# Folds on VectorE, four transposes a tile, smaller code and pair steps, and another passage between two passes

## The chip, the cores and the metric

The kernel runs on one core of one Trainium2 chip. The metric is the device time of one execution in microseconds (us); the time of a kernel is the median of its runs.

## What is computed

The input x holds 16 x 1024 = 16384 tokens of E = 512 numbers (f32). Cut to what matters:

```python
xn = layernorm(x)                                   # over the 512 numbers
# attention part: a circular filter, a 24-bit code, its correction
D    = fractal_dimension(xn)                        # from the first 1024 numbers
x1   = ifft(fft(xn) * wave_filter(D, E)).real
bits = sigmoid(x1 @ W_el + b_el) > 0.5              # 24 bits a token
syn  = (bits @ H.T > 0.5); w = syn.sum(-1)          # 12 checks
corrected = bits with the pattern of syn flipped if 0 < w <= 3
s    = x1 + corrected @ W_le + b_le
# expert part: top 2 of 8 experts
probs   = softmax(xn @ router_w.T)
v, idx  = top_k(probs, 2)
weights = v / (v.sum() + 1e-6)
f    = sum over the two of (xn @ expert_w[idx] + v) * weights
out  = x + s * silu(f)
```

## The kernel before, in words

Tokens are cut into NT = 128 tiles of 128 tokens. The kernel passes over them twice.

**First pass** (`pass_1`, a loop over tiles g). Blocks of TPT = 4 tiles (1 MB) are loaded by SP (`load_block`, L157) into a pool `xin` of 5 buffers, AHEAD_L = 16 tiles ahead. The circular filter has mirror symmetry, so a row is first folded: `fold` (L442 to L450) adds and subtracts the halves of a row (L445, into `halved`, with the second quarter written mirrored) and then subtracts two quarters (L448, into `folded`). The list `folds` says in which tile each of a block's three fold steps is issued, on VectorE (DVE). `transpose` (L528, L532) turns the folded rows on TensorE (PE): two pairs of transposes at L528 add up in PSUM, which does one more sum of quarters, and two at L532 turn `folded`; ScalarE (ACT) copies the result to `pmt` (L534). `filt` multiplies `pmt` with the filter `fw` (L542, four f32 matmuls of 128x162), ACT copies the filtered tile to `yb` (L548), and SP stores a block of them to `yd` (L556). `take` reduces the 34 small columns (24 latents, 8 logits, two sums) to `raw` (L472, DVE, one a tile). `spread` squares the row with a sum on ACT (L459). PE turns tile g+1 ahead of the filter of tile g.

Small operations follow the tiles. For each group of GT = 8 tiles `scale` (L488 to L510) works out mean and scale of the layernorm on DVE, ACT and one POOL copy; `code` (L567 to L622) forms the bits, turns them on PE (L576), gets the checks by a matmul (L585), corrects the first 12 bits and packs them into one integer. For each round of RT = 16 tiles `route` (L654 to L825) finds the two experts, their weights and bias, marks the pair among 28 (`pair`, L729, four products), counts tokens of each pair before this one by matmuls, and so the place of each token in its pair's list (L782, L787); then POOL (GpSimd) scatters one record a token to `lists` in DRAM (L791). These operations wait in Python lists (`scales`, `now`, `routes`, `rest`, `aside`); `pass_1` issues about one from each at fixed places in a tile, between the folds. `None` in a list skips a turn. After SOON = 80 tiles `whole_ops(0)` (L873 to L944) reads the lists of the first 30 whole tiles back.

**The passage.** `lead_x` (g = 118), `lead_normal` (g = 124) and `lead_turn` (g = 127) prepare the second pass's first tile inside the first pass. After the last tile come the last `take` and the last `scale`. Then the pools of the first pass close, and those of the second take their memory.

**Second pass** (a loop over n from -11). Tokens are now sorted by pairs of experts: 101 "whole" tiles of one pair each, 61 "item" tiles of one expert each for what is left over, 27 "rest" tiles that put these together. POOL gathers x and the filtered rows (`fetch_x`, `fetch_y`, L1082); `normalize` (L1267, DVE); then the tile is turned, the first six on PE (`turn`, L1276, copy L1278), the others by ACT copies and a DMA (L1283 to L1292). `product` (L1324) is four f32 matmuls of 128x512; a whole tile has two, one an expert, joined by `scaled` (L1381, ACT) and `added` (L1384 DVE, L1387 ACT). The corrected code goes through `triple` (L1339, L1340, DVE: a bit mask to 3 x 32 numbers), `turn_code` (L1354 PE, L1358 ACT) and `mend` (L1366 PE); `spread_out` (L1371 to L1378) unfolds the filtered row; `combine` (L1423, L1424) makes the output, which POOL scatters (`put`, L1433). The order is written out by hand: a table `due` says in which turn n of the loop each step of tile k is issued, all but the products in `beside`, which runs between the two products of a tile.

## Time and profile before

| what | us |
|---|---|
| median of 5 runs | 1384.13 |
| lowest and highest | 1370.68, 1396.9 |
| the profiled execution | 1377.58 |
| its span on the core | 1375.7 |
| PE busy | 1246.8 (91%) |
| DVE busy | 998.5 (73%) |
| ACT busy | 787.9 (57%) |
| POOL busy | 796.0 (58%) |
| last `raw` (L472) of the first pass starts | 302.70 |
| first product (L1324) starts | 312.79 |
| third product starts | 322.4 |

A group in the profile is written: line, engine, operation, output <- input by the program's names, partitions x elements, how often; then its busy time and the mean ns of one; then the idle time of its engine just before it and who ended that. PEld is the loading of PE's weights, which overlaps PE. "issue" is time in which an engine waited for nothing that the profile shows. The granted clock is the share of full speed that TensorE's throttle allowed. A chain of waits follows the end back through what released each step.

### The profile page before, as it was taken

To read this page: it belongs to the slowest core of one execution; us is meant where nothing else is said; L and a number is where in the kernel's file an instruction comes from. 1 tells how busy PE (TensorE), PEld (TensorE's weight loads), DVE (VectorE), ACT (ScalarE), POOL (GpSimd) and SP (SyncE) were. 2 spreads that over 40 slices of the span, in tenths; PEclk is the share of its full clock that TensorE was granted. 3 is DMA by queue.
4 is the path that set the end of the run, shared out by engine and by line. 5 is a ranking of instruction groups with operands and counts; after the bars stand their busy time and mean duration, and the time that the engine had idled before them with its cause. 6 is when DMAs were issued, how large, how long until landed. Compare 5 with 4: busy or idle time off the path is not lost.

```text
span 1375.7 us, 17149 instructions
## 1 busy us (share of the span) xinstructions
PE 1246.8 (91%) x4417; PEld 685.6 (50%) x4417; DVE 998.5 (73%) x2538; ACT 787.9 (57%) x1326; POOL 796.0 (58%) x764
## 2 busy tenths in 40 slices
PE   9999886967897999988989998999899999996997
PEld 8988886853342444433434433444344444442444
DVE  8899886763865799633323444699798999995996
ACT  7988886763433454554545555456465555553553
POOL 0065555346475375654566543577767777776761
PEclk9999999998898999998999999999999999997998
DMA  8888786544345465775788889779877798886871
GB/s 304 296 288 281 271 277 220 181 165 124 77 124 131 102 167 131 185 189 141 179 200 208 198 194 188 194 186 220 220 193 218 195 214 212 212 211 181 211 195 62
DMA packets 235640, 266.42 MB, mean 194 GB/s; under 512 B 182558, under 2 KB 183070, under 8 KB 227482
## 3 DMA queue, kind: packets, MB, share of 16 engines
q1 hardware_dynamic: 188330, 133.16, 37.9%
q0 software_dynamic: 46928, 132.03, 33.2%
q8 instruction: 40, 0.66, 0.2%
q14 instruction: 54, 0.44, 0.1%
q10 hardware_dynamic: 288, 0.13, 0.0%
HBM read 140.79 MB, written 83.56 MB: 163 GB/s over the span
## 4 chain that ended last, share of the span: by engine, by line
PE 37%; DVE 21%; issue 18%; POOL 7%; another core or an unknown queue 6%; DMA 5%; ACT 4%; SPq 0%; POOLq 0%; DVEq 0%; ACTq 0%
PE pe L1324 26%; PE py L542 6%; DMA plt<-pl 3%; DVE acc L1384 3%; DVE halved L445 2%; DVE yg L1371 2%; POOL xg L1082 2%; PE pt L528 2%; POOL entry L1082 2%; POOL out L1433 2%; DVE yg L1423 2%; DVE xn L1267 1%; DVE mix L1374 1%; PE pt L532 1%
## 5 line engine op out<-in xcount | busy, mean ns | idle before, releaser
L1324 PE MATMUL pe<-w_sb,xt 128*128 x2136 | 953.1, 599 | 28.8 <-ACT xt L1292 8.0
L1324 PEld LDWEIGHTS pe<-w_sb,xt 128*128 128x128 f32 x2136 | 408.1, 194 | 505.4 <-issue 455.8
L1292 ACT COPY xt<-plt 128x1024 uint16<-128x1024 uint16 x156 | 209.3, 1342 | 87.0 <-DMA plt<-pl 58.2
L791 POOL DMA_INDIRECT lists<-rec,dst x128 | 143.5, 1121 | 99.3 <-issue 67.9
L1387 ACT ACTIVATE acc<-acc,stats 128x512 f32<-128x512 f32 (+2 forms) x103 | 73.5, 714 | 217.6 <-DVE acc L1384 174.3
L542 PE MATMUL py<-fw,pmt 128*128 128x162 f32 x1024 | 169.5, 308 | 29.3 <-ACT pmt L534 16.7
L1433 POOL DMA_INDIRECT out<-xg,toks x100 | 112.1, 1121 | 131.1 <-DVE xg L1424 102.8
L542 PEld LDWEIGHTS py<-fw,pmt 128*128 128x128 f32 x1024 | 146.8, 192 | 39.7 <-ACT pmt L534 21.3
L1283 ACT COPY pl<-xn 128x1024 uint16<-128x1024 uint16 x156 | 162.0, 1038 | 0.0
L1384 DVE SCALAR_TENSOR_TENSOR acc<-pe,stats,acc 128x512 f32<-128x512 f32 (+2 forms) x103 | 75.9, 737 | 117.9 <-remote 52.7
L1395 DVE COPY part<-pe 128x512 f32<-128x512 f32 x61 | 42.0, 689 | 152.6 <-remote 82.1
L1082 POOL DMA_INDIRECT yg<-yd,toks x101 | 112.4, 1113 | 69.7 <-DVE xg L1424 26.6
L1381 ACT ACTIVATE acc<-pe,stats 128x512 f32<-128x512 f32 (+2 forms) x103 | 68.9, 669 | 119.5 <-remote 49.2
L1082 POOL DMA_INDIRECT xg<-in_x,toks x100 | 109.6, 1096 | 45.6 <-issue 31.1
L548 ACT COPY yb<-py 128x512 f32<-128x512 f32 x128 | 75.5, 590 | 35.0 <-PE py L542 14.2
L459 ACT ACTIVATE no<-xt 128x512 bf16<-128x512 f32 x128 | 92.5, 723 | 0.0
L1423 DVE TENSOR_TENSOR yg<-yg,acc 128x512 f32<-128x512 f32 (+1 forms) x130 | 87.9, 676 | 5.2 <-ACT acc L1387 5.2
L1424 DVE TENSOR_TENSOR xg<-yg,xg 128x512 f32<-128x512 f32 (+1 forms) x129 | 88.2, 684 | 4.5
L1082 POOL DMA_INDIRECT part<-ed,adr_r x54 | 61.0, 1130 | 40.8 <-DVE mix L1375 20.6
L445 DVE TENSOR_TENSOR halved<-xt 128x512 f32<-128x512 f32 (+1 forms) x136 | 82.7, 649 | 0.1
L534 ACT COPY pmt<-pt 128x512 f32<-128x512 f32 x128 | 73.9, 577 | 12.0 <-remote 5.9
L1082 POOL DMA_INDIRECT entry<-lists,adr_i x61 | 63.2, 1036 | 28.4 <-issue 18.3
(279 smaller groups left out, 1483.2 us busy)
## 6 DMA issues: line engine op xcount, KB each, us to landing
yd<-yb SPq DMA_DIRECT2D x32, 1024.0 KB
xt<-in_x SPq DMA_DIRECT2D x31, 1024.0 KB
ed<-part SPq DMA_DIRECT2D x61, 256.0 KB
w_sb<-in_expert_w SPq DMA_DIRECT2D x32, 256.0 KB
plt<-pl SPq DMA_TRANSPOSE x156
lists<-rec,dst POOLq DMA_INDIRECT x128
yg<-yd,toks POOLq DMA_INDIRECT x101
xg<-in_x,toks POOLq DMA_INDIRECT x100
```

What stands on the lines that cost most here:

```text
L445: op(to[:, :, ::-1] if q else to, x[:, :, a:z], x[:, :, H + a : H + z])
L459: nc.scalar.activation(no, x, AF.Square, bias=x[:, 0:1], scale=-1.0, accum_out=k.sq2[:, j : j + 1],)
L542: nc.tensor.matmul(blocks(py)[:, i // 2, i % 2, :], pmt[:, i, :], fw[:, i, :], start=True, stop=True,)
L791: dma = nc.gpsimd.indirect_dma_start(out=lists, out_offset=bass.IndirectOffsetOnAxis(ap=st.dst[:, j : j + 1], axis=0), in_=st.rec.bitcast( ...
L1082: nc.gpsimd.indirect_dma_start(out=dst, out_offset=None, in_=src, in_offset=bass.IndirectOffsetOnAxis(ap=idx, axis=0), bounds_check=limit - 1,
L1283: nc.scalar.copy(k.pl.rearrange("p (h e) -> p h e", h=2), k.xn.bitcast(U16).rearrange("p (e h) -> p h e", h=2),)
L1292: nc.scalar.copy(k.xt.bitcast(U16).rearrange("p c (t h) -> p h c t", h=2), k.plt.rearrange("p (h c) t -> p h c t", h=2),)
L1324: nc.tensor.matmul(pe[:, o].unsqueeze(1), k.xt[:, c, :], w_sb[:, bass.ds(e, 1), c, o], start=(c == 0), stop=(c == KC - 1),)
L1384: nc.vector.scalar_tensor_tensor(k.acc[:, c], src[:, c], k.w1, k.acc[:, c], ALU.mult, ALU.add)
L1423: nc.vector.tensor_mul(k.mix[:, c], k.mix[:, c], k.acc[:, c])
L1424: nc.vector.tensor_add(k.x[:, c], k.mix[:, c], k.x[:, c])
L1433: dma = nc.gpsimd.indirect_dma_start(out=of, out_offset=bass.IndirectOffsetOnAxis(ap=k.tok, axis=0), in_=k.x, in_offset=None, bounds_check ...
```

## The change

- **Folds.** Sum and difference of the halves are one operation each for a block (128x1024 instead of two of 128x512), not mirrored any more; the difference of quarters reads its second input mirrored; a fourth operation adds the quarters in place, which the two pairs of transposes did before. `transpose` is four plain ones. A block's folds are issued in four tiles.
- **Groups.** GT is 16, so scale, code and route all work on 16 tiles. `xin` has 4 buffers and loads are issued 12 tiles ahead. SOON is 64. Constants made on the chip (`iota_e`, `rev`) come as rows.
- **Code.** The matmul of the checks has a 13th column that gives the code word as a number; the checks are weighted so that their sum holds count and pattern; the correction is an exclusive or of two integers a token.
- **Route.** Equality with the largest and the rank are one operation; the pair comes from a sum of two marks compared with 28 keys (one `is_equal` of 128x448) instead of four products; the matrix of the rank has 2^22 on its diagonal, so that the place is a maximum instead of a product and a sum; the weights take fewer operations.
- **Budget.** A tile gets a credit of 2.1 (us) less 0.21; folds and small operations take from it, and small operations are issued while some is left.
- **Passage.** The triples of the first four tiles are formed in the first pass's last four tiles. The last group's scale moves from the end of the first pass to turn n = -5, behind `normalize` of the second tile, with its MEAN copy on ACT. `turn` of tile k is due at k - 1 (before: max(k - 3, min(k - 2, 3))), `turn_code` at max(k / 2, k - 3), with half turns placed between the second product and `added`. Every 15th gathered x uses the first tile's buffer.

```diff
-    SOON = 80
+    SOON = 64
-    xin = p1.enter_context(tc.tile_pool(name="xin", bufs=5))
+    xin = p1.enter_context(tc.tile_pool(name="xin", bufs=4))
...
-    GT = 2 * TPT
+    GT = 4 * TPT
-    AHEAD_L = 16
-    RT = 2 * GT
+    AHEAD_L = 12
+    STEP, LATE = 2.1, 2.1
+    RT = GT
...
         if i < 2:
             op = nc.vector.tensor_sub if i else nc.vector.tensor_add
-            for q in range(2):
-                a, z = q * Q, (1 + q) * Q
-                to = t[:, :, i * H + a : i * H + z]
-                op(to[:, :, ::-1] if q else to, x[:, :, a:z], x[:, :, H + a : H + z])
+            op(t[:, :, i * H : (i + 1) * H], x[:, :, 0:H], x[:, :, H:E])
         else:
             v = t.rearrange("p j (a h n) -> p j a h n", a=2, h=2)
-            nc.vector.tensor_sub(
-                h.rearrange("p j (a n) -> p j a n", a=2), v[:, :, :, 0, :], v[:, :, :, 1, :]
-            )
+            if i == 2:
+                nc.vector.tensor_sub(
+                    h.rearrange("p j (a n) -> p j a n", a=2), v[:, :, :, 0, :], v[:, :, :, 1, ::-1]
+                )
+            else:
+                nc.vector.tensor_add(v[:, :, :, 0, :], v[:, :, :, 0, :], v[:, :, :, 1, ::-1])
...
         for c in range(2):
-            for i, half in enumerate((t[:, c, 0, :], t[:, c, 1, :])):
-                nc.tensor.matmul(
-                    pt[:, c, :], half, ident, start=(i == 0), stop=(i == 1), is_transpose=True
-                )
+            nc.tensor.transpose(pt[:, c, :], t[:, c, 0, :], ident)
...
         def c0():
             o.syn = made("syn", 12)
-            nc.vector.tensor_scalar(o.syn, k.pg, 0.5, None, ALU.is_gt)
+            nc.vector.scalar_tensor_tensor(
+                o.syn, k.pg[:, :, 0:12], 0.5, worth_r.unsqueeze(1).to_broadcast([P, GT, 12]),
+                ALU.is_gt, ALU.mult,
+            )
...
         def c2():
+            o.word = made("word", 0, I32)
+            nc.vector.tensor_copy(o.word, k.pg[:, :, 12])
         def c3():
+            o.fix = made("fix", 0, I32)
+            nc.vector.scalar_tensor_tensor(o.fix, o.w, 4.0 * COUNT, o.w, ALU.is_lt, ALU.mult)
+        def c4():
+            nc.vector.tensor_scalar(o.fix, o.fix, COUNT - 1, None, ALU.bitwise_and)
+        def c5():
+            nc.vector.tensor_tensor(
+                k.rec.bitcast(I32)[:, :, BITS], o.fix, o.word, ALU.bitwise_xor
+            )
...
+        def pairs_():
+            st.oh = new("oh", [P, S, NPAIR], BF16)
+            v.tensor_tensor(
+                st.oh,
+                st.key.unsqueeze(2).to_broadcast([P, S, NPAIR]),
+                key_r.unsqueeze(1).to_broadcast([P, S, NPAIR]),
+                ALU.is_equal,
+            )
...
+        def where():
+            st.far = new("far", [P, S])
+            v.tensor_reduce(st.far, st.pk, AX.X, ALU.max)
         def place():
-            st.pl = new("pl", [P, S, NPAIR])
-            v.tensor_mul(st.pl, st.pk, st.oh)
...
+        def small_ops(n):
+            nonlocal credit
+            for _ in range(n):
+                going = False
+                for ops in (scales, routes, now):
+                    if credit <= 0 or not ops or ops[0] is None or id(ops) in waiting:
+                        continue
+                    if ops[0]() is False:
+                        waiting.add(id(ops))
+                        continue
+                    credit -= getattr(ops.pop(0), "us", 0.17)
+                    going = True
+                if not going:
+                    break
...
+            credit = min(credit, 0.4) + (STEP if g < NT - 16 else LATE) - 0.21
+            waiting.clear()
+            small_ops(1)
             while folds and folds[0][0] <= g:
-                fold(*folds.pop(0)[1:])
+                b, i, js = folds.pop(0)[1:]
+                fold(b, i, js)
+                credit -= 1.2 * (js.stop - js.start) / TPT
                 steps(rest, 1)
...
+            small_ops(99)
...
+            if g >= NT - 4:
+                n = len(lead.b3)
+                lead.b3.append(triple_of(masks[0][:, n : n + 1]))
...
-        for op in scales + scale(NG - 1):
+        for op in scales:
             op()
...
+        pool, name = (xgp, "xg") if (k.at - 1) % (XG + 1) else (own, "x0")
...
         "turn": [
-            None if crossed[k] else max(k - AHEAD_T, min(k - 2, 3)) for k in range(NTILE)
+            None if crossed[k] else k - 1 for k in range(NTILE)
         ],
-        "turn_code": [k - 3 for k in range(NTILE)],
+        "turn_code": [max(k / 2, k - 3) for k in range(NTILE)],
...
             each(n + AHEAD_N, normalize)
+            if n + AHEAD_N == 1:
+                for op in scale(NG - 1):
+                    if op:
+                        op()
```

## The prediction

> **What bounds the kernel now.** I read the page's forty slices first, then tables of busy time by stretch, then the groups of instructions by form inside a steady stretch, then the waits and the chain around the passage. The change touches the first pass and the few tiles after it, so the first question is who sets the pace there. Columns of the table: stretch and its length, then busy us (and instructions) of PE, PEld, DVE, ACT, POOL, then PE's granted clock, DMA share, GB/s.
>
> ```profile
> 16.00:45.00 29.00, 28.38 (x222) 27.29 (x221) 26.24 (x70) 27.71 (x67) 0.42 (x2) 1.00 0.85 318
> 45.00:145.00 100.00, 92.32 (x712) 86.99 (x711) 91.18 (x319) 89.27 (x228) 42.87 (x40) 1.00 0.85 289
> 145.00:217.00 72.00, 64.08 (x487) 59.59 (x486) 62.15 (x214) 60.14 (x154) 40.08 (x37) 1.00 0.80 272
> 217.00:265.00 48.00, 37.48 (x257) 33.93 (x256) 35.22 (x126) 31.08 (x78) 18.75 (x19) 0.89 0.59 205
> 265.00:303.00 38.00, 28.93 (x213) 25.99 (x211) 25.52 (x96) 28.15 (x72) 18.02 (x18) 1.00 0.34 119
> ```
>
> The same table of L472 alone (one instruction a tile) counts tiles: 16, 48, 32, 17, 16. So a tile takes 1.81, 2.08, 2.25, 2.82 and 2.38 us in the five stretches. In the second, PE, DVE and ACT are each busy 89 to 92 of 100: no engine alone is the bound, three that hand work to each other are. DMA moves 289 GB/s there and 318 in the stretch before, so it is not at its end. In the last two everything is slack: 33 tiles take 86 us where 2.08 each would be 69. The steady stretch by form:
>
> ```profile
> L542 PE MATMUL py<-fw,pmt 128*128 128x162 f32 x384 | 62.5, 305 | 5.3 <-ACT pmt L534 1.8 <-DVE dev L515 1.2 <-DVE athot L679 1.0
> ...
> L445 DVE TENSOR_TENSOR halved<-xt 128x512 f32<-128x512 f32 x49 | 31.4, 680 | 0.0
> L528 PE MATMUL pt<-ident,halved 128*128 128x128 f32 x190 | 29.0, 274 | 0.0
> ...
> L532 PE MATMUL pt<-ident,folded 128*128 128x128 f32 x96 | 18.3, 273 | 0.0
> ...
> L448 DVE TENSOR_TENSOR folded<-halved 128x1024 f32<-128x1024 f32 x12 | 14.6, 1216 | 0.0
> L472 DVE TENSOR_REDUCE raw<-py 128x34 f32<-128x136 f32 x48 | 14.1, 294 | 3.4 <-ACT yb L548 2.3 <-issue 1.1
> ```
>
> PE's idle time falls before the filter (L542), behind ACT and behind DVE's small operations; DVE has next to no idle time ahead of its folds. The passage, in the chain of waits:
>
> ```profile
> 301.98 6.26 DMA xg<-in_x,toks
> ...
> 311.56 0.85 PE pt L1276 x4
> 312.42 0.11 PE pc L1354
> 312.52 0.27 issue
> 312.79 5.79 PE pe L1324 x8
> ```
>
> and in the list of waits from 300 to 320:
>
> ```profile
> POOL xg L1082 <- ACT no L459: 14.1, 1, 14.1
> ...
> PE pc L1354 <- DVE b L1340: 8.7, 1, 8.7
> ```
>
> The last filter ends near 302, then PE stands 8.7 us, although its first product needs only tile 0, turned already: in PE's order tile 1's transposes and code words stand ahead of it. The rest, 312.8 to 1365, is products (L1324, 953 of the 1052 us), which the diff leaves alone past the first tiles.
>
> **The change part by part.** Profiled execution: 1377.6 us (span 1375.7 and 1.9 around it); the median of five is 1384.1, 0.5% above. I take gains against the former and set them off from the latter.
>
> *Folds on DVE.* A block of four tiles had four of 128x512 (680 ns) and one of 128x1024 (1216). It gets four of 128x1024. Neighbours on DVE overlap by about 0.08 us in the timeline (two L445 take 1.22, not 1.36). Before: 4 x 0.680 + 1.216 - 5 x 0.08 = 3.54; after: 4 x 1.216 - 4 x 0.08 = 4.54. So +1.00 a block, +4.0 us for 16 tiles. The mirrored read now sits on an input; the mirrored write of L445 shares a 1.22 us pair with a plain one, so I cost mirroring at nothing (bounds 0 to +0.2 us an operation).
>
> *Small operations on DVE, for 16 tiles, by rows.* Scale: two rounds of seven (0.170 + 0.174 + 0.162 + 0.159 + 0.136 + 0.166 + 0.419 = 1.39) become one with six of 0.17 and a 128x512 of 0.68: 2.77 to 1.70. Code: two of 2.01 (L567 to L622) become one of 0.55 (384 elements, from 351 ns at 192 and the folds' slope of 1.05 ns an element), 0.35, 0.35 and four of 0.17: 4.02 to 1.93. Route: 10.2 to 7.85; gone are the four pair products (0.88) for one is_equal of 128x448 (0.61), three operations of 0.28, one 0.61 product, seven of 0.17. Sum 17.0 to 11.5, and some 30 instructions fewer. Start to start (less 0.08 where they overlap) that is 13.0 to 8.6: -4.3 us, against +4.0 of the folds. DVE per tile stays where it was, 1.90 us, and -0.02 (bounds -0.06 to +0.06).
>
> *Transposes.* Six a tile become four. A steady tile's four L528 take 0.60 us and two L532 0.38 in the timeline, so one costs 0.11; PE falls by 0.22 us a tile, 1.94 to 1.72. ACT: half the scale and spread steps, -0.03 of 1.86.
>
> *What that makes of the pace.* 2.08 us is 0.14 above the busiest engine, because three are level. Now PE is 0.2 below, with DVE 1.89 and ACT 1.83 left. Lower bound 1.89 (DVE never waits); upper bound 2.08 (the waits for L548 and for dependent pairs stay). I take 2.00, since PE's own waits for DVE and ACT no longer pass on: -0.08 on 112 tiles = -9. The first sixteen, with no small operations, are DVE's loss: 26.24/16 = 1.64 + 0.25 = 1.89 against 1.81, with waits +2, and +0.5 in the setup's extra fold. In the slow stretches (23 us over 2.08 a tile) PE's lighter tile saves a sixth, -4. First pass: -11 (bounds -25, the slow stretches gone; +5, below).
>
> *Group of 16, credit.* One scale for 16 tiles comes at most 8 tiles later, records and scatters with it. POOL is busy 43 of 100 in the steady stretch, so its queue of scatters, the same 128, absorbs that; each is one L791 of 1.1 us. In code and scale the empty steps give PE and ACT a tile each, so waits like DVE's 3.7 us for L502 (six of 0.6) should go: inside the 2.00. The last group has no successor in the first pass; its scale now runs on DVE behind the second normalise, 1.2 us where DVE waits for gathers anyway (3.65 us at 308), and its MEAN copy moves from POOL's queue (0.22 between gathers) to ACT. POOL's order is else the same: 8 xg gathers, 6 yg, then the scatters.
>
> *Loads.* Blocks are issued 12 tiles ahead, not 16, with four buffers, so the slack before the first fold falls from 11 to 7 tiles: 14 us against a landing of some 7. Cover: that slack. If a landing takes over 14 us, DVE waits.
>
> *SOON 64.* The read-back of the lists comes 16 tiles earlier; 30 whole tiles are full there either way. Same operations: nothing.
>
> *Passage.* Tile 1's turn moves behind the first product; tile 0 to 3's masks (0.44 us each) go to the last four tiles, where DVE is busy 25.5 of 38. The first product then starts at the end of pass 1 (302.7) + 0.3, not +10.1; the second waits for turn(1): gather landed +6.3, normalise 0.65, transposes and copy 1.2, about +8; the third at +11.6, where it was at 322.4, +19.7. So -8. Later forward waits change place: normalise(6) now stands behind turn(2), a product later, and the third product's psum behind the first addition; -1 to +2. The stall from 326.5 (9.2 and 4.7 us on the chain, PE's completions late with no named cause) may go or stay: 0, bounds -14 and 0. I take -9 with the first product at full clock (3.6, not 5.79, while the second may pay that).
>
> The granted clock was 0.70 from 302.7 to 312.8, behind PE's 8.7 us stand, and the four matmuls of the first product took 3.78 us of 5.79 in their first half. [...]
>
> Sum: -11 - 9 = -20: 1357.6 by the profiled execution, 1364 by the median.
>
> **The rivals.**
> *DVE sets the pace, so fewer transposes buy nothing.* For: DVE is 91 of 100 busy already and gains nothing net. Against: its waits are on L548, behind PE. The pace stays 2.08, and only the passage (-9) and -1 remain: 1374.
>
> *The passage gives nothing.* Second and third product wait for something else (a psum buffer, the 326.5 stall grown by what was saved). For: 18% of the chain is issue time and 6% unnamed. Pass 1's -11 stays: 1373.
>
> *Slower: DVE's whole-block folds hold up the reduce.* Each fold is one 1.22 us instruction in three of four tiles before and in all four now; behind it stand L472 and the small operations, and PE's next filter waits for L472 to free py, of which there are two. If each fold makes the filter wait, a tile costs DVE's 1.89 plus the reduce's own chain, filter 1.27 to L548 0.59 (1.86 in series, half of it beside DVE at best): up to 2.3 us. It decides from where the pace passes 2.08 + 9/112 = 2.16; at 2.30 pass 1 costs +25, with the passage +16: 1400. For: L472's 3.4 us of waits are on that chain now. Against: in the second stretch, three of four tiles already hold 1.2 us of folds with PE 92% busy.
>
> *The slow stretches go.* 23 us in pass 1 and 14 in the passage stand over the pace; if they hang on PE being full, half more leaves: 1342.
>
> **How the numbers follow.** Chances: forecast 0.45 (1354 to 1373), DVE bound 0.18, no passage 0.11, slower 0.15, slow stretches gone 0.11. About 1% (14 us) is what the runs, 1371 to 1397, can tell from none: faster is below 1370, slower above 1398. Forecast's part under 1370 is 0.36 of 0.45, the last case 0.11, and 0.06 of the two middle ones: 0.53. Slower: 0.6 of its rival 0.15 and 0.04 of mishaps in the long second pass: 0.13. Same: 0.34. The range, 1343 to 1396, leaves out half of the last case and half of the slower one with a little. The forecast's own range is 1354 to 1373.
>
> **What would show it.** Steps of L472: 2.00 us a tile from 45 to 217, and about 1.9 in 16 to 45. Folds x128 at 1.22. Of the small operations some 30 fewer for 16 tiles. Four transposes taking 0.60, PE busy near 82 of 100, DVE over 92. DVE's waits for xt: none. First L1324 within 1 us of the last filter, third 12 us behind it, and pass 1's last L472 near 292. Wrong if L472's pace is 2.08 or more, if DVE waits for loads, if the third product still comes 19 us after the pass, or if the second pass (1053 us from first product to end) has changed length by more than the passage's share.

## The result: 0.8% slower, and the profile after

The changed kernel takes 1384.8 us (median of 52 runs, 1367 to 1403); the kernel before took 1378.0 beside it (94 runs, 1355 to 1403). The ratio is 1.0079, interval 1.0058 to 1.0099: about 11 us slower (6.8 by the medians), where 20 faster were forecast. Here and below a ratio and its interval go by the runs within about 1.5% of the kernel's fastest alone, a median by all runs, so that the two can differ (most for the old passage with early folds, where three of twelve runs count). The profiled execution has a span of 1383.6 us, 7.9 above the one of before.

By stage the profiles differ thus: the first pass ends (last `raw`) at 317.6 instead of 302.7, +15, and from there to the end it is 1066 us instead of 1073, -7. So the passage paid about as forecast, and the first pass, which was to end at 292, lost 15 where it should have gained 11. Busy time by stretch, of the kernel after (columns as before; the stretches hold 16, 32, 32, 16 and 24 tiles, and the last 8 tiles follow them):

```profile
18.30:52.50 34.20, 28.61 (x197) 26.68 (x197) 29.84 (x60) 26.91 (x65) 0.24 (x1) 0.95 0.61 225
52.50:123.00 70.50, 56.46 (x414) 51.08 (x414) 61.43 (x156) 58.73 (x146) 23.62 (x21) 1.00 0.77 273
123.00:197.00 74.00, 60.21 (x414) 55.18 (x413) 61.74 (x157) 59.21 (x146) 39.97 (x34) 0.93 0.74 262
197.00:248.50 51.50, 37.45 (x225) 33.66 (x225) 33.46 (x88) 29.94 (x74) 20.94 (x17) 0.80 0.54 186
248.50:297.00 48.50, 41.10 (x305) 37.78 (x304) 45.31 (x116) 43.58 (x111) 29.47 (x24) 1.00 0.82 272
```

The loads came out as worked out: in the second row DVE is busy 61.43/32 = 1.92 us a tile, PE 56.46/32 = 1.76. But a tile takes 2.20 us there and 2.31 in the next row, where the same 32 tiles took 2.08 and 2.23 before. DVE is 87% busy, not over 92: no engine is full, so the loss is waiting. Whose? Take the first pass as a whole, from the first `raw` to its end. Before, the kernel's row was

```profile
15.90:302.70 286.80, 251.29 (x1882) 233.90 (x1879) 240.12 (x822) 236.35 (x594) 119.84 (x114) 0.98 0.73 251
```

and after

```profile
18.30:318.00 299.70, 237.86 (x1636) 216.72 (x1635) 244.37 (x623) 231.40 (x571) 124.57 (x104) 0.94 0.68 238
```

PE works 13.4 us less and stands 61.8 us instead of 35.5: 26 us more of waiting swallow the lighter work and add 13; the other 2.4 of the 15 lie ahead of the first `raw`. The groups of the first pass, by form, say where PE stands; of the kernel after:

```profile
L532 PE MATMUL pt<-ident,halved 128*128 128x128 f32 x256 | 54.0, 295 | 37.7 <-DVE halved L455 24.8 <-DVE dst L801 4.8 <-DVE lohi L719 3.5
...
L477 DVE TENSOR_REDUCE raw<-py 128x34 f32<-128x136 f32 x128 | 37.6, 294 | 39.0 <-ACT yb L550 29.9 <-issue 8.6
```

and the same two operations before:

```profile
L528 PE MATMUL pt<-ident,halved 128*128 128x128 f32 x512 | 78.8, 277 | 0.0
...
L472 DVE TENSOR_REDUCE raw<-py 128x34 f32<-128x136 f32 x128 | 37.6, 294 | 32.6 <-ACT yb L548 21.3 <-issue 10.9
```

The first transposes of a tile never waited before; now PE stands 37.7 us in front of them, two thirds of it for L455, the new fourth fold (the quarters added in place). One such wait, in the timeline:

```profile
90.53 1.21 DVE L455 TENSOR_TENSOR halved<-halved 128x1024 f32<-128x1024 f32 x1
...
91.89 0.41 PE L532 MATMUL pt<-ident,halved 128*128 128x128 f32 x2 [1.85 <-DVE halved L455]
...
92.56 0.58 ACT L536 COPY pmt<-pt 128x512 f32<-128x512 f32 x1 [1.06 <-issue]
...
94.28 0.30 DVE L477 TENSOR_REDUCE raw<-py 128x34 f32<-128x136 f32 x1 [0.99 <-ACT yb L550]
```

The fold ends at 91.74, PE starts 0.15 later after standing 1.85, ACT's copy starts behind that, and 2.5 us after the fold DVE itself stands 0.99 in front of its reduce, behind ACT's copy of the filter's result: the wait goes round all three engines. PE waits so for L455 18 times in the pass. The fold is late because it is due in the last tile before the one in which PE turns its block, and the code and route operations stand ahead of it in DVE's order.

The passage, of the kernel after:

```profile
317.98 3.70 PE L1350 MATMUL pe<-w_sb,xt 128*128 x8 [1.14 <-DVE raw L477]
...
323.81 0.66 PE L1302 MATMUL pt<-ident,xn 128*128 128x128 f32 x4 [2.12 <-issue]
...
324.36 5.39 PE L1350 MATMUL pe<-w_sb,xt 128*128 x8
```

The first product starts 0.4 us after the last `raw` (10.1 before), the third 12.0 after it (19.7 before, 11.6 forecast), the ninth 57.5 (63.2).

### The profile page after: what moved, and what is told of

The parts are those of the page before. It is cut to its first block, busy times and chain, and to the rows that moved or that the text cites. A ratio compares the mean times of both kernels' runs of the same rounds, so it can differ in the third digit from the quotient of the medians.

```text
span 1383.6 us, 16291 instructions
## 1 busy us (share of the span) xinstructions
PE 1235.2 (89%) x4161; PEld 669.4 (48%) x4161; DVE 997.8 (72%) x2311; ACT 781.0 (56%) x1301; POOL 805.2 (58%) x747
## 4 chain that ended last, share of the span: by engine, by line
PE 41%; DVE 28%; issue 11%; another core or an unknown queue 7%; DMA 5%; POOL 3%; ACT 3%; SPq 1%; POOLq 0%; DVEq 0%; ACTq 0%
PE pe L1350 34%; PE py L544 3%; DVE acc L1402 3%; DMA plt<-pl 3%; DVE yg L1389 3%; DVE halved L447 2%; DVE yg L1443 2%; DVE halved L455 2%; DVE folded L451 2%; DVE xn L1293 2%; DVE mix L1392 2%; DVE yg L1395 1%; POOL out L1453 1%; DVE yg L1396 1%
## 5 line engine op out<-in xcount | busy, mean ns | idle before, releaser
L805 POOL DMA_INDIRECT lists<-rec,dst x128 | 152.7, 1193 | 119.8 <-issue 79.3
L544 PE MATMUL py<-fw,pmt 128*128 128x162 f32 x1024 | 178.8, 320 | 22.5 <-ACT pmt L536 11.2
L544 PEld LDWEIGHTS py<-fw,pmt 128*128 128x128 f32 x1024 | 155.5, 202 | 30.9 <-ACT pmt L536 17.3
L1402 DVE SCALAR_TENSOR_TENSOR acc<-pe,stats,acc 128x512 f32<-128x512 f32 (+2 forms) x103 | 75.9, 736 | 113.1 <-remote 36.7
L1094 POOL DMA_INDIRECT yg<-yd,toks x101 | 110.6, 1095 | 63.2 <-DVE xg L1444 23.3
L1094 POOL DMA_INDIRECT xg<-in_x,toks x94 | 103.6, 1102 | 36.6 <-issue 28.1
L532 PE MATMUL pt<-ident,halved 128*128 128x128 f32 x256 | 54.0, 295 | 37.7 <-DVE halved L455 24.8
L1444 DVE TENSOR_TENSOR xg<-yg,xg 128x512 f32<-128x512 f32 (+2 forms) x121 | 82.6, 683 | 4.2
```

Of the source, the lines that this page charges most:

```text
L544: nc.tensor.matmul(blocks(py)[:, i // 2, i % 2, :], pmt[:, i, :], fw[:, i, :], start=True, stop=True,)
L805: dma = nc.gpsimd.indirect_dma_start(out=lists, out_offset=bass.IndirectOffsetOnAxis(ap=st.dst[:, j : j + 1], axis=0), in_=st.rec.bitcast( ...
L1094: nc.gpsimd.indirect_dma_start(out=dst, out_offset=None, in_=src, in_offset=bass.IndirectOffsetOnAxis(ap=idx, axis=0), bounds_check=limit - 1,
L1402: nc.vector.scalar_tensor_tensor(k.acc[:, c], src[:, c], k.w1, k.acc[:, c], ALU.mult, ALU.add)
L1444: nc.vector.tensor_add(k.x[:, c], k.mix[:, c], k.x[:, c])
```

## The experiments

The kernel before took 1383, 1418, 1280, 1379 and 1280 us beside the five groups of runs, on five chips, so each run is given as its ratio to the kernel before on the same chip, and medians are compared inside a group only.

### Is the fourth fold too late?

*Folds one tile earlier.* In the kernel after:

```diff
-            (4 * b + i - 5, b, i, slice(0, TPT)) for b in range(2, NB) for i in range(4)
+            (4 * b + i - 6, b, i, slice(0, TPT)) for b in range(2, NB) for i in range(4)
```

> The changed kernel with every fold step of a block due one tile earlier (4b+i-6 instead of 4b+i-5), nothing else. Theory F (the fourth fold step, L455, ends in the tile just before PE turns the block, so PE stands behind DVE): the idle time of L532 behind DVE falls from some 37 us to under 8, the pace in the middle of the first pass from 2.28 to about 2.0-2.1 us a tile, and the time by 10 to 25 us, to 0.985-0.995 of before. Rival D (DVE simply carries too much, 1.92 us a tile, and the order does not matter): PE waits as long elsewhere, time within 4 us of the changed kernel, 1.005-1.01 of before. Rival G (an emptier PE is clocked down): pace hardly moves and the granted clock stays below 0.95 between 120 and 250 us.

Measured: 1374.8 us, 0.9979 (0.9935 to 1.0022); first pass ends at 302.3 in its profile. Against the 1.0079 of the change that is 1% less. PE's wait in front of L532 is down to 2.4 us, as theory F says, but the time lies between the ranges of F and D. Theory G is not shown: the granted clock of the profile's slices is 0.7 from 203 to 237 us, as the change's is from 208 to 242, and 0.9 or more in the other slices of the first pass of both.

*Folds one tile later in the kernel before*, whose last fold then ends where the new one does (`4 * b + i - 5` becomes `- 4`):

> The kernel before with its three fold steps due one tile later (4b+i-4), so that its last step ends where the changed kernel's does; six transposes, old small operations. Theory F: PE now waits for L448 at every block, 10 to 30 us in all (0.6 before), and the time grows by 8 to 20 us, 1.006-1.015. Rival D: DVE's load is as before, so the time is within 0.4% of before.

Measured: 1394.5 us, 1.0115 (1.0070 to 1.0161), first pass to 326.0. In the first 310 us PE stands 25.1 us for the last fold, 0.2 in the kernel before:

```profile
L532 PE MATMUL pt<-ident,folded 128*128 128x128 f32 x244 | 49.2, 284 | 25.5 <-DVE folded L448 25.1 <-issue 0.4
```

The old folds and six transposes lose as much as the whole change when their last fold is due where the new one is. So the due time costs about 1% in both kernels, whichever folds are made.

*Old folds and six transposes in the kernel after*, with the credit and the new passage kept:

```diff
-        for i in range(4):
+        for i in range(3):
...
-            nc.tensor.transpose(pt[:, c, :], t[:, c, 0, :], ident)
+            for i, half in enumerate((t[:, c, 0, :], t[:, c, 1, :])):
+                nc.tensor.matmul(
+                    pt[:, c, :], half, ident, start=(i == 0), stop=(i == 1), is_transpose=True
+                )
...
-            (4 * b + i - 5, b, i, slice(0, TPT)) for b in range(2, NB) for i in range(4)
+            (4 * b + i - 5, b, i, slice(0, TPT)) for b in range(2, NB) for i in range(3)
```

> The changed kernel with the folds and six transposes of before (five fold operations a block in three steps, due as before), but the smaller code and route, groups of 16, budget and new passage kept. DVE then has 0.25 us a tile less than before. Theory F: no fold is late, and the three engines share the load: 0.98-0.99 of before (passage -8, small operations -5 to -15). Rival D: the same gain, since DVE is lighter; it differs from F only together with the first run. Rival: budget and grouping cost time themselves: 1.00 or above.

Measured: 1386.8 us, 1.0053 (1.0006 to 1.0100), first pass to 323.0. Here no fourth fold exists, and the kernel is still no faster than before, as the last rival said. Something else in the change costs as well.

### The passage alone, and the read-back

*The new passage in the kernel before*, the first pass untouched but for the four masks:

```diff
-            None if crossed[k] else max(k - AHEAD_T, min(k - 2, 3)) for k in range(NTILE)
+            None if crossed[k] else k - 1 for k in range(NTILE)
...
-        "turn_code": [k - 3 for k in range(NTILE)],
+        "turn_code": [max(k / 2, k - 3) for k in range(NTILE)],
...
+            if g >= NT - 4:
+                n = len(lead.b3)
+                lead.b3.append(triple_of(masks[0][:, n : n + 1]))
```

> The kernel before with the new passage alone: turns due at k-1, code words at max(k/2, k-3) with half turns, the first four triples and the last group's scale moved as in the change; the gathers keep their 14 buffers. From the two profiles the passage gains about 10 us (third product 12 us behind the first pass instead of 19.7, later products up to 10 ahead): 0.992-0.995 of before. Rival: the gain is a matter of where unnamed late completions fall, then 0.998-1.002.

Measured: 1390.0 us, 1.0122 (1.0055 to 1.0190) in six runs, outside both ranges. In its profile the ninth product starts 58.0 us after the first pass (63.2 before), so the passage itself is shorter, yet the runs are slower. The first pass ends 3.6 us later than before, at 306.3, though the edit leaves it alone but for the four masks.

*The old passage in the kernel after with early folds* (due times, masks and the last scale put back):

```diff
-        for op in scales:
-            op()
+        for op in scales + scale(NG - 1):
+            if op:
+                op()
...
-            None if crossed[k] else k - 1 for k in range(NTILE)
+            None if crossed[k] else max(k - AHEAD_T, min(k - 2, 3)) for k in range(NTILE)
```

> The changed kernel with folds a tile earlier and the old passage (turns, code words, triples and the last group's scale where the kernel before has them; the 15th gather buffer stays). The new passage alone took the kernel before to 1.012 [1.006, 1.019], though its profile shows later products 5 us nearer to the first pass's end. If the passage really costs time, this kernel is 0.5 to 1.5% faster than the one with early folds (0.998): 0.985-0.993. If the passage gains its 5 us and the 1.012 came from elsewhere (a chance of where late completions fall), it is 0.3-0.5% slower: 1.000-1.003.

Measured: 1415.8 us, 0.9913 (0.9842 to 0.9985). *SOON back at 80*, early folds (`SOON = 64` becomes `80`), on the same chip:

> The changed kernel with folds a tile earlier and SOON = 80 again. Theory: with SOON = 64 DVE stands 9 to 13 us for the read-back of the lists (ttf <- tt, L924), since POOL's scatters lag behind the tiles; with 80 the wait is absent as in the kernel before, and the time falls by 6 to 12 us, to 0.988-0.994. Rival: the wait moves 16 tiles on with the read-back and is paid there: 0.995-1.001.

Measured: 1414.5 us, 1.0008 (0.9966 to 1.0049). The medians of the two are 1.4 us apart. Against the early folds of the first group (0.9979) the read-back's place is within the intervals: worth nothing, as forecast. The wait moves with it, as the rival said: DVE stands 9.7 us for the gather, and the long round of 16 tiles is the one from tile 96 (48.3 us) instead of the one from tile 80. On the passage the ratios lean against the gain, but their intervals overlap.

*The new passage on top of new folds*, in pairs on one chip. The base is the kernel before with the four new folds, due one tile early, and four transposes:

> The kernel before with the new folds, due a tile earlier, and four transposes, once more, as anchor for the three beside it. It stood at 0.981 [0.974, 0.988] of before; if that holds on another chip, 0.975-0.99. If it was a chance of that chip, 0.995 or above.

Measured: 1292.5 us, 1.0116 (1.0079 to 1.0153). With the passage's edit of above added:

> The same as the anchor, with the new passage. On the two other bases the new passage cost 0.7% (0.998 against 0.991) and 1.2%. If it costs by itself, this is 0.7-1.2% above the anchor; if its 5 us nearer products count, 0.3-0.5% below it.

Measured: 1287.2 us, 1.0059 (1.0035 to 1.0083): 5.3 us less by the medians, 0.6% by the ratios. The ninth product starts 45.9 us after the first pass instead of 54.8. This pair, with the narrowest intervals (they still overlap a little), gives the passage 5 to 7 us. Why it lost in the first group is not settled.

### What the folds and the loads cost by themselves

*The same kernel on another chip*, the one on which the kernel before took 1418 us:

```diff
-            for i, half in enumerate((t[:, c, 0, :], t[:, c, 1, :])):
-                nc.tensor.matmul(
-                    pt[:, c, :], half, ident, start=(i == 0), stop=(i == 1), is_transpose=True
-                )
+            nc.tensor.transpose(pt[:, c, :], t[:, c, 0, :], ident)
...
-            (4 * b + i - 5, b, i, slice(0, TPT)) for b in range(2, NB) for i in range(3)
+            (4 * b + i - 6, b, i, slice(0, TPT)) for b in range(2, NB) for i in range(4)
```

> The kernel before with the new folds (four operations of 128x1024 a block, the first due at 4b-6) and four transposes, all else as before: small operations in groups of 8, old passage. DVE's work grows by 0.25 us a tile from 1.90 to 2.15, PE's falls by 0.22. If DVE's total sets the pace, it is 2.2-2.3 us a tile, 10 to 20 us slower: 1.007-1.015. If PE's relief counts for more, 0.99-1.00; then the smaller code and route were not needed to pay for the folds.

Measured: 1390.1 us, 0.9806 (0.9736 to 0.9876). One kernel, 1.9% faster than before on one chip and 1.2% slower on another: these two do not agree, and I have no reason for it from the profiles; none was taken of the kernel before on a chip where it takes 1280 us. The second reads plainly. Of `b_folds4_again`, 64 tiles:

```profile
49.80:187.50 137.70, 117.08 (x828) 103.93 (x827) 135.85 (x409) 119.50 (x305) 67.16 (x58) 1.00 0.81 282
```

2.15 us a tile with DVE busy 98.7%: four folds beside the old small operations fill DVE, and PE's lighter tile (1.83 us busy, 1.92 in the kernel before from 45 to 145) buys nothing. The fewer small operations are what pays for the fold.

*Four buffers, 12 tiles ahead*, on top of that:

```diff
-    xin = p1.enter_context(tc.tile_pool(name="xin", bufs=5))
+    xin = p1.enter_context(tc.tile_pool(name="xin", bufs=4))
...
-    AHEAD_L = 16
+    AHEAD_L = 12
```

> The same with the loads of the change: 4 buffers of x, blocks issued 12 tiles ahead instead of 16. Theory L (the slack lost to the fourth fold step makes loads come late, so that folds wait and PE with them): 8 to 15 us slower than the anchor, 0.6-1.1%. Rival: the slack of six tiles (12 us) still covers a landing of about 7, and the time is within 0.3% of the anchor.

Measured: 1292.5 us, 1.0104 (1.0072 to 1.0135), the same as without. The loads' slack covers them, as forecast.

### The credit

*Early folds, old passage, no credit*: small operations go out at the fixed places of the kernel before, around the tile's fold.

```diff
-            credit = min(credit, 0.4) + (STEP if g < NT - 16 else LATE) - 0.21
-            waiting.clear()
-            small_ops(1)
+            one_route()
+            one(scales)
+            one_route()
+            one(now)
...
+            one(now)
+            one_route()
+            one(scales)
+            one_route()
+            one(now)
...
-            small_ops(99)
```

> The changed kernel with early folds and the old passage (0.991 of before), its small operations issued as the kernel before does, one from each list at four fixed places in a tile, without the credit. Theory B (credit pushes code and route of 16 tiles into two of a round's four blocks, where DVE then holds up the reduce and PE, blocks of 8.5 and 8.7 up to 16 us against 6.7): the load is spread and the time falls by 0.5-1%, to 0.981-0.987. Rival: what costs is that code and route of 16 tiles come together at all, or their operations; then 0.988-0.995.

Measured: 1270.4 us, 0.9931 (0.9908 to 0.9954), and 128 us for the 64 tiles from 46 to 174: 2.00 a tile, the forecast's pace. The ratio is in the rival's range and no better than the 0.9913 with the credit, which was measured on another chip, so by the time theory B is not confirmed. The pace pointed at the credit all the same, so the next group crosses the two suspects on one chip, all four with the new passage. The change as it is, again:

> The changed kernel itself, as anchor beside the three others. 1.006-1.010 of before, if the first measurement holds on this chip.

Its early folds, again:

> The changed kernel with the folds a tile earlier, nothing else, once more. Theory F: 0.8-1.3% below after_again, and PE's wait for L455 gone (37 us of waits for DVE before L532 in the changed kernel). If the credit is the larger part, less than 0.5% below.

Without the credit (the diff above), folds as changed:

> The changed kernel without the credit, folds late as in the change. If the credit only costs where the folds are late (it puts small operations ahead of the fold), this is 0.5-1% below after_again; if lateness alone counts, within 0.3% of after_again.

Without the credit and with early folds:

> Folds a tile earlier, small operations issued without the credit, new passage. From 0.993 for the same with the old passage, and 0.57% for the passage measured beside it on one chip (1.0059 against 1.0116): 0.985-0.990, a pace of 2.0 us a tile, faster than both kernels. Rival (the passage costs, as 1.012 for it alone said): 0.995-1.002.

Measured, the kernel before at 1379.1 us:

| | folds as changed | folds one tile earlier |
|---|---|---|
| credit of 2.1 | 1386.7, 1.0125 (1.0073 to 1.0178) | 1377.8 (six runs of 1351 to 1392), no ratio |
| no credit | 1359.9, 0.9873 (0.9819 to 0.9927) | 1340.2, 0.9756 (0.9703 to 0.9809) |

The credit costs 27 us by the medians with late folds, and the two intervals lie far apart; the late fold costs 20 without the credit. The other two differences, 38 for the credit with early folds and 9 for the late fold with the credit, rest on the six runs of the upper right kernel, which spread over 40 us, and are weak. First passes end at 315.1, 311.8, 300.5 and 288.7 us. So with late folds only 14.6 us of the credit's cost lie in the first pass (315.1 to 300.5). The rest of the profiled execution is 15.6 us shorter without the credit as well, 1054.9 us instead of 1070.5, in operations that the edit leaves alone; why is not shown. For the late fold without the credit the two parts are 11.8 and 5.1 us. Both suspects are real, the credit is the larger, and the lower right kernel beats both kernels by 2.4% or more.

Each leaves its own mark. The first transposes' idle time in the first 300 us, of the change again, of its early folds, without the credit, and without both:

```profile
L532 PE MATMUL pt<-ident,halved 128*128 128x128 f32 x249 | 51.0, 287 | 40.3 <-DVE halved L455 26.0 <-DVE dst L801 4.8 <-DVE lohi L719 4.3
```

```profile
L532 PE MATMUL pt<-ident,halved 128*128 128x128 f32 x254 | 51.1, 284 | 2.5 <-DVE halved L455 2.5
```

```profile
L532 PE MATMUL pt<-ident,halved 128*128 128x128 f32 x256 | 52.1, 286 | 44.1 <-DVE halved L455 40.1 <-remote 1.7 <-PE py L544 1.6
```

```profile
L532 PE MATMUL pt<-ident,halved 128*128 128x128 f32 x256 | 51.3, 282 | 4.4 <-DVE halved L455 2.7 <-DVE word L612 1.5
```

Folds one tile earlier take this wait from 40 to 44 us down to 3 or 4, with and without the credit. But the second kernel of the four has no wait there and is still slow. Its rounds of 16 tiles:

```profile
49.30:80.40 31.10, 29.10 (x213) 26.37 (x212) 30.23 (x80) 28.86 (x74) 2.21 (x2) 1.00 0.89 320
80.40:119.00 38.60, 32.43 (x204) 28.39 (x203) 30.93 (x79) 29.64 (x74) 18.34 (x18) 0.87 0.69 242
119.00:158.80 39.80, 31.60 (x208) 28.56 (x207) 30.99 (x80) 29.62 (x74) 17.98 (x18) 0.91 0.71 242
```

against those of the kernel with neither:

```profile
49.70:82.10 32.40, 29.67 (x212) 26.25 (x211) 30.70 (x79) 28.97 (x74) 5.43 (x6) 1.00 0.86 307
82.10:114.30 32.20, 29.12 (x207) 25.62 (x206) 30.80 (x78) 29.02 (x74) 20.93 (x18) 1.00 0.83 295
114.30:146.60 32.30, 29.42 (x208) 25.82 (x207) 30.85 (x79) 29.07 (x74) 21.04 (x18) 1.00 0.88 303
179.60:226.10 46.50, 33.42 (x222) 29.78 (x221) 34.14 (x93) 29.07 (x74) 23.10 (x19) 0.85 0.60 204
```

With the credit the first round is even faster, 31.1 us, and the next two take 38.6 and 39.8 for the same instructions; without it all are 32.3. Executions differ: in the profile of the same kernel from the first group (1357.7 us) the three take 31.1, 40.4 and 32.1. In the slow rounds some steps come late behind PE with no engine of the core named (`issue` or `remote` in the brackets), PE stands, and the granted clock falls: in the row 80.40:119.00 it is 0.87, 1.00 up to 94 and 0.50 from 96 to 106. There PE's pairs of transposes take 0.63 us instead of 0.38. PE's transposes, the copy of them and the next filter:

```profile
92.10 0.38 PE L534 MATMUL pt<-ident,folded 128*128 128x128 f32 x2
94.25 0.59 ACT L536 COPY pmt<-pt 128x512 f32<-128x512 f32 x1 [0.47 <-remote]
94.88 1.61 PE L544 MATMUL py<-fw,pmt 128*128 128x162 f32 x8 [2.41 <-issue]
```

The transposes end at 92.48 by their record. ACT has other work until 93.78 and copies them at 94.25, and the filter comes after a stand of 2.41 us for which no engine is named. The filter after it, at a clock of 0.50, takes 2.53 us; the one at 90.61, at 1.00, took 1.37.

Such steps are not a mark of the credit alone. The kernel before has them in its slow stretch from 217:

```profile
228.40 0.58 ACT L534 COPY pmt<-pt 128x512 f32<-128x512 f32 x1 [3.04 <-remote]
...
236.90 2.53 PE L542 MATMUL py<-fw,pmt 128*128 128x162 f32 x8 [5.84 <-ACT pmt L534]
```

There too the clock is 0.50, from 235 to 245. The kernel before with folds one tile later, and with the new passage alone, has them as well, in its first pass. All profiles with such steps come from chips on which the kernel before takes 1378 us or more; the seven from the two chips where it takes 1280 have none of 1.4 us or more in the first pass. On the chip of the four above, both kernels with the credit have steps that come 2 us late or more (the change itself one, at 309) and the two without it have none. And the change loses in its middle rounds without any: tiles 32 to 80 take 36.4, 38.3 and 36.7 us a round, without the credit 33.9, 33.8 and 34.4. What starts the late steps, and by what else the credit costs, the traces don't say.

*A larger credit*, early folds, new passage:

```diff
-    STEP, LATE = 2.1, 2.1
+    STEP, LATE = 2.6, 2.6
```

> The changed kernel with folds a tile earlier and a credit of 2.6 instead of 2.1 us a tile. If the credit is simply too small (0.69 us a tile left for small operations beside a fold; with 2.6 it is 1.19), the rounds of tiles 32 to 80 fall from 38-40 us to 32-33, and the time to 0.976-0.985 of before, as without the credit. If it is the order in which the credit puts the operations, 0.995-1.002 as with 2.1.

Measured: 1277.0 us, 0.9967 (0.9944 to 0.9990), in the range of the second theory, though its rounds are 33 us long and without late steps, as the first says; its first pass ends at 295.3. It ran on a chip on which the kernel before takes 1280 us, and on those no profile has late steps and no kernel with the credit of 2.1 was run. So that the larger credit is rid of them is not shown. With early folds and no credit a first pass ended at 285.3 on the other chip of that kind (third group, old passage). So some 10 us of the credit's cost stay with 2.6, and late steps are no part of them.

### What remains in the best kernel

*The read-back's copy seven tiles later*, on the kernel with neither. In the row 179.60:226.10 above 16 tiles take 46.5 us, 14 over the pace; there the waits name DVE's copy of the lists and, behind it, PE:

```profile
PE py L544 <- DVE raw L477: 11.1, 1, 11.1
DVE ttf L924 <- DMA tt<-lists,idx: 9.5, 1, 9.5
```

```diff
-        aside.extend([experts, None, fetch] + [None] * 5 + [apart, None, None, turned, None, kept])
+        aside.extend([experts, None, fetch] + [None] * 12 + [apart, None, None, turned, None, kept])
```

> Early folds, no credit, new passage (0.976), and twelve empty steps instead of five between the read-back's gather and DVE's copy of it. If DVE's wait for that gather (9.5 us, PE stands 11) is the 14 us that the round of tiles 80 to 96 takes over the others, it falls from 46.5 to 33-36 us and the time by 9 to 12 us, to 0.966-0.970. If POOL's lag grows with the distance, 0.974-0.978.

Measured: 1255.4 us, 0.9813 (0.9778 to 0.9848); that round falls to 35.3 us, DVE's wait to 1.4. The ratio is outside both ranges, which start from the 0.976 of another chip, and the kernel without this edit was not run on this one; but its first pass ends at 274.1, and with the old passage and the early copy it ended at 285.3 on the other chip of this kind, 11 us later. So the long round from tile 80 in the kernels with groups of 16 (51.4 us in the change, where the wait is 9.3) is mostly DVE standing in order behind a gather, and PE behind DVE. The slow stretch that the prediction saw in the kernel before is another: it is the round from tile 96 (47.5 us), DVE does not wait for the gather there at all, and its marks are the late steps and the clock of 0.50 shown above.

*No credit, old folds, six transposes*, new passage, read-back as changed, on the same chip:

> The changed kernel without the credit, with the folds of before in three steps and six transposes, new passage. PE 1.94 us a tile, DVE 1.66. From the rows, the pace is PE's 1.94 and a little, 2.0: level with four transposes (2.02), so 0.973-0.980 of before, and the change's main part is worth nothing by itself. If PE full to the brim costs as it did before, 2.08-2.1 and 0.982-0.988: then it is worth 8 us.

Measured: 1257.7 us, 0.9804 (0.9776 to 0.9832). 64 steady tiles of it, PE 98.6% busy:

```profile
45.60:169.40 123.80, 122.09 (x952) 115.75 (x950) 108.53 (x331) 116.84 (x292) 61.05 (x56) 1.00 0.93 312
```

and of the kernel with four transposes and the later copy, DVE 96% busy:

```profile
49.00:177.50 128.50, 117.52 (x830) 103.56 (x829) 123.60 (x317) 115.98 (x293) 67.59 (x56) 1.00 0.88 302
```

1.93 us a tile with six transposes, 2.01 with four. The two kernels are even only because the second is rid of most of the read-back's wait; the first still has 7.0 us of it, and a round of 45.5 us. So four transposes and all folds on VectorE, the change's first part, lose 0.07 us a tile, some 8 us in 112 tiles, once nothing else is in the way (by one profile of each). Six transposes, no credit and the later copy together were not run, and the smaller operations and the groups of 16 were not run apart.

## Why the prediction was wrong, step by step

- **"Group of 16, credit ... inside the 2.00"** failed. It was costed at nothing, with the empty steps expected to remove waits. In the crossed runs the credit costs 27 us with late folds, 14.6 of them in the first pass, and with a larger one some 10 us of the first pass stay. What it costs by is not settled: late steps go with it in some executions, and the change loses in rounds without them. That an order of issue can cost was not bounded; it should have had both ends, as it moves every small operation on the fullest engine.
- **The rival of the late fold was the right fear on the wrong chain.** It let the folds hold up the reduce, and was set aside since "three of four tiles already hold 1.2 us of folds with PE 92% busy". What matters is not how many folds there are but when the last one ends: PE's idle time in front of the transposes went from 0.0 to 37.7 us, 24.8 of it for the fourth fold, and moving the folds one tile takes it down to 2.4. The sum named no term for PE waiting for a fold; it took the pace down to 2.00 because PE's waits "no longer pass on", and 2.20 to 2.31 was measured. The late fold costs some 20 us where it was measured best, without the credit.
- **The durations and loads held.** Folds 1215 to 1220 ns each (1.22 forecast), four transposes, DVE 1.92 a tile (1.89) and PE 1.76 (1.72). The pace of 2.00 is what the kernel runs at with early folds and no credit, 128 us for 64 tiles: the sum described a kernel whose order is right. Four slips in the working change nothing of this: two L445 take 1.28 or 1.29 us in most pairs, which is the overlap of 0.08, and 1.22 only in some, PE's 92.32 us for 48 tiles are 1.92 a tile and not 1.94, the savings listed for route leave 7.3 and not 7.85 us of its 10.2, and half of the 37 us of slow stretches off 1364 is 1345 and not 1342.
- **"DVE sets the pace, so fewer transposes buy nothing"**, a rival at 0.18, is what the mended kernels show: DVE 96% busy at 2.01, where the six transposes run at 1.93. The forecast took 2.00 as a gain over 2.08; the gain is that of fewer small operations, and the transposes give some of it back.
- **First sixteen tiles and setup**: +2.5 forecast, measured +2.4 to the first `raw` and +5 in the sixteen tiles, with 3.5 of it PE's wait for L455.
- **Slow stretches** (-4 forecast): nothing of it came. No row showed that PE's work sets the time there. Before, the long round is tiles 96 to 112, 47.5 us, with late steps and a clock of 0.50; after, it is tiles 80 to 96, 51.4 us, with 9.3 us of DVE's wait for the read-back's gather, which the kernel before does not have.
- **Passage** (-9): the first product at +0.4 and the third at +12.0 came as forecast (+0.3, +11.6): 7.7 of the 8 us are there at the third. By the ninth the gain is 5.7 us, by the rest of the profile 7, by the timed pair 5 to 7. What is missing is lost behind the third product: the fourth starts 7.5 us after it, 4.4 before, and PE stands 2.9 of them for the addition (`added`, L1402), a wait that the prediction gave -1 to +2. The second product was the slow one, 5.39 us against 3.70 of the first, at a granted clock of 0.70, but it started at +6.8 instead of +8, which made up for it:

```profile
318.00:322.00 4.00, 3.68 (x8) 1.42 (x8) 0.00 (x0) 0.22 (x1) 3.03 (x3) 1.00 0.91 322
...
324.30:330.00 5.70, 5.70 (x13) 2.47 (x12) 3.38 (x8) 2.10 (x7) 4.48 (x5) 0.70 0.74 211
```

  PE stood only 2.1 us in front of the second product's transposes here, where the prediction's own starts (+0.3, a product of 3.6, then +8) leave about 4. In `b_folds4_pass`, behind a stand of 2.15, the second product ran in 3.69: a stand of that length was followed by a slow product in one execution and not in the other. What makes it slow is not shown.
- **Loads and SOON** (nothing each): both hold.
- **Range and chances.** The range of 1343 to 1396 held the time by its width; the sign was wrong. The slower rival (+25 in the first pass, where +15 was measured) was nearer than the forecast (-11), and had 0.15 of the chance.

## What to carry to other kernels

When work moves to another engine, sum its load and then ask when the last piece ends against when its consumer starts: here one tile of lead was worth 20 us of 1360. An order of issue, a budget or credit above all, is a change of its own, to be run alone: the credit cost 27 us here with late folds. And when three engines are level, taking work from one and giving it to the fullest needs the fullest to get more room than it is given: here DVE was 96% busy at 2.01 us a tile, where the six transposes ran at 1.93.

## What the runs showed that was not expected

- Steps that come 2 us or more behind PE's recorded end with no engine named (the two timelines above, each followed by some 10 us at a granted clock of 0.50) go with rounds of 38 us and more where others take 31 to 33. They stand in profiles with and without the credit, all of them from chips on which the kernel before takes 1378 us or more. Cause open.
- The kernel before took 1280 us on two chips and 1379 to 1418 on three. In the one kernel that can be compared the first pass has little part in it: with early folds and no credit it ends at 285.3 us on a chip of the former kind and at 288.7 on one of the latter, while the rest takes 987 and 1050 us (old passage on the former, new on the latter).
- The sign of one edit differed between two chips: the four folds alone gave 0.9806 on one and 1.0116 on the other. What caused it is open.
- The same waiting goes with two clocks: from 52.5 to 123 of the kernel after, PE stands 14 us, at most 1.8 at a time, and the granted clock is 1.00; from 197 to 248.5 it stands 14 us again, 7.3 of them in one piece, and the clock is 0.80. Over the first pass the clock is 0.94 against 0.98 before. A matmul of the filter (L544) lasts 320 ns there instead of 308, and the 1024 of them keep PE busy for 178.8 us instead of 169.5, which is most of why PE's work fell by 13.4 us and not by the 28 that the forecast's 0.22 a tile would give.
